# One grid operation ahead of the context's division on VectorE, and x's evictions swapped between VectorE and ScalarE

## The chip, the cores and the metric

The kernel runs on one core of a Trainium2 chip. The metric is the device time of one execution in microseconds, the median over the runs. Engines: TensorE (PE; PEld is its weight load), VectorE (DVE), ScalarE (ACT), GpSimd (POOL), and SyncE (SP), which here issues most DMAs.

## The reference

Four layers follow each other on x, 8 batches of 512 x 512 in float32. The change lies in the second, and moves operations of the first that run inside it:

```python
# L0: a finite-difference step on the 512 x 512 grid of each batch
df = -gradv_Af + gradvv_Bf * 0.5
f_new = jnp.maximum(f + df * dt[:, None, None], 0.0)
# L1: a transformer block, 16 heads of 32
x = _ln(src) * (1.0 + scale) + shift
scores = einsum(q / sqrt(32), k) + attention_bias, masked with -inf
ctx = einsum(softmax(scores), v)
x = x + (ctx @ Wo + bo);  h = _ln(x) * g2 + beta2
x = x + _gelu2(h @ W1 + b1) @ W2 + b2
# L2: an expert's MLP per batch with layer norm;  L3: a low-rank response, gated
```

## The kernel before

The program has three stages: the grid step of batch 0 (up to about 65 us), the attention of all batches (up to about 1165 us), and the MLPs with the low-rank layer. The change lies in the attention stage (`attention_stage`, lines 522 to 1097).

The attention works in 128 units (b, c, r): batch b, a group c of four heads, and a quarter r of the query rows (row index modulo 4). A batch has 16 units; the texts count them from 0 to 15 in their batch (t = 4c + r). The loop of line 1060 runs over units and overlaps three of them: `now` is in its softmax, `old` (the unit before) has its probabilities transposed, and `two` (the one before that) has its context summed. Every instruction of the compute engines is pinned to the order of the program, so that the order on an engine is that of the code; the bias loads on SyncE are not pinned and a scheduler places them.

What one turn of the loop issues, in order:

- on GpSimd a gate (L713), a tiny addition that reads the last grid operation's output and so holds GpSimd back until VectorE is through with the grid operations of the turn before; then two additions of the mask to the next unit's bias (L945);
- `turned` (L979) and `softmax` (L961), twice: transposes of the probabilities into a PSUM tile tr, copied to pt by VectorE (L993) for the first head and by ScalarE (L995) for the second; then on VectorE scores plus bias with the row minimum (bt, mn, L968), on ScalarE the exponential (L973). Between them lie pieces of the job that `fill` (L879) gives to this unit: a block of q, k, v or of the output projection, four matmuls at a time;
- the rest of the job. In unit 9 of a batch this holds `x1_in` (L578) four times, for the next batch: TensorE transposes a 128-column block c of the normalised x into a PSUM tile xtr, and it is evicted to SBUF as x1 with scale and shift, on ScalarE (L587) for even c and on VectorE (L589) for odd c;
- every fourth turn (units 1, 5, 9 and 13, for the head group that ended two units ago) `divide` (L1019): TensorE transposes the reciprocals of the sums (rb), ScalarE copies them out (rbs, L1024), VectorE multiplies the context with them (ct, L1027). Each turn then has `inverse` (L1012), the reciprocals of the unit `old` (rs on VectorE, rw on ScalarE);
- the bias loads three units ahead (L934), then the grid operations of this turn (`grid_sums`, L803), then the coefficient loads of the grid (`grid_loads`, L696) on SyncE;
- the score matmuls of the next unit (L950).

The tiles tr, xtr, rb and xb (the transposes back) share two PSUM banks (tag "tr"), so a transpose waits until an earlier tile of its bank has been evicted.

The grid step of batch n runs during batch n-1's attention, from its unit 8 on. Its place is a table by hand, `GRID` (L797): for each step j the names of the operations. A letter is a coefficient or an action and a digit the half (two of each partition's four rows): e0 multiplies the coefficient tile e of half 0 with f on VectorE, C0 adds c0 to the sum, and so on; each is a tensor_tensor of 128x1024 in SBUF (L664). Only n0 and n1 (the layer norm) put passes on ScalarE, two each (L791). Step j of batch n falls in turn i = 16(n-1) - 8 + j, so the turns with a division are the steps 1, 5, 9 and 13. The coefficients are loaded two to four units ahead: e0 at step -1, g0 at step 1, e1 at step 6, a1 at step 9.

Of the kernel before, what the change touches and what calls it, by code (L numbers as in the profile page):

```python
# [24 lines left out]
R = 4  # L25
# [496 lines left out]
def attention_stage(  # L522
# [13 lines left out]
    with ExitStack() as ctx:  # L536
# [9 lines left out]
        def tp(out, src):  # L546
            pin(nc.tensor.transpose(out, src, ident))  # L547
# [30 lines left out]
        def x1_in(b, c):  # L578
            tag, bufs = ("tr", 2) if b or c < 2 else (f"s{c}", 1)
            tr = ps.tile([P, R, P], F32, name=f"xtr_{b}_{c}", tag=tag, bufs=bufs)  # L580
            for r in range(R):
                tp(tr[:, r, :], xt[b][:, r, c * P : (c + 1) * P])
            t = io.tile([P, S], F32, name=f"x1_{b}_{c}", tag="x1", bufs=4)
            tv, trv = t.rearrange("f (p r) -> f p r", r=R), tr.rearrange("f r p -> f p r")
            g, h = sc1[:, c, b : b + 1], shift[:, c, b : b + 1]
            if c % 2 == 0:
                pin(nc.scalar.activation(tv, trv, AF.Identity, bias=h, scale=g))  # L587
            else:
                pin(nc.vector.tensor_scalar(tv, trv, g, h, ALU.mult, ALU.add))  # L589
            x1s[b, c] = t  # L590
# [117 lines left out]
        def grid_gate(i):  # L708

            t = gs.pop("last", None)  # L710
            if t is not None:
                g = small.tile([P, 1], F32, name=f"gate_{i}", tag="gate", bufs=2)
                pin(nc.gpsimd.tensor_tensor(g, t, t, ALU.add))  # L713

        def grid_ghosts(n):
            f = gs[n, "f"]
            m1 = small.tile([P, R, 2, 4], F32, name=f"m1_{n}", tag="gm1", bufs=1)
            m2 = small.tile([P, R + 2, 2, 3], F32, name=f"m2_{n}", tag="gm2", bufs=1)

            def times(out, x, y):  # L720
                pin(nc.vector.tensor_tensor(out, x, y, ALU.mult))

            for i in range(2):
                o = 508 * i
                times(m1[:, :, i, :], grid["gab"][:, :, i, :], f[:, 1 : R + 1, o : o + 4])
                o = 509 * i
                times(m2[:, :, i, :], grid["gte"][:, :, i, :], f[:, :, o : o + 3])
            e1 = small.tile([P, R, 2], F32, name=f"e1_{n}", tag="ge1", bufs=2)
            e2 = small.tile([P, R + 2, 2], F32, name=f"e2_{n}", tag="ge2", bufs=1)
            pin(nc.vector.tensor_reduce(e1, m1, AX.X, ALU.add))  # L730
            pin(nc.vector.tensor_reduce(e2, m2, AX.X, ALU.add))
            gv(e1, e1, e2[:, 2 : R + 2, :], ALU.add)
            gv(e1, e1, e2[:, 0:R, :], ALU.subtract)
            gs[n, "ghost"] = e1

        def grid_op(n, op):
# [46 lines left out]
            elif key == "n":  # L783
# [5 lines left out]
                for r in range(2):  # L789
# [4 lines left out]
                        )  # L794
                    )

        GRID = {  # L797
            0: "q0 q1", 1: "e0", 2: "w0 c0 hh", 3: "C0", 4: "+0 -0", 5: "g0", 6: "G0 a0",
            7: "A0 b0 B0", 8: "x0 q2", 9: "e1 w1 c1", 10: "C1 +1", 11: "-1 g1", 12: "G1 s0",
            13: "n0 a1 A1 b1", 14: "B1 x1", 15: "s1", 16: "n1",  # L800
        }

        def grid_sums(n, j):  # L803
            for op in GRID.get(j, "").split():
                if op == "hh":
                    grid_ghosts(n)
                else:
                    grid_op(n, op)
# [6 lines left out]
        def grid_step(i, f):  # L815
            for n in range(1, NB):
                j = i - (16 * (n - 1) - 8)
                if -2 <= j <= 16:
                    f(n, j)
# [55 lines left out]
        def grid_early(j):  # L875
            grid_sums(1, j)
            grid_loads(1, j)
# [63 lines left out]
        def add_mask(b, c, r):  # L941
            for u in range(2):
                bt = bias[b, c, r, u]
                pin(
                    nc.gpsimd.tensor_tensor(  # L945
                        bt, bt, mask[b, r][:, None, :].to_broadcast([P, 2, S]), ALU.add
                    )
                )
# [12 lines left out]
        def softmax(b, c, r, u):  # L961

            bt = bias[b, c, r, u]
            for i in range(2):
                h = 2 * u + i
                mn = small.tile([P, 1], F32, name=f"mn_{b}_{c}_{r}_{h}", tag=f"mn{h}")
                pin(
                    nc.vector.tensor_tensor_reduce(  # L968
                        bt[:, i, :], ss[h], bt[:, i, :], -1.0, 3.0e38, ALU.add, ALU.min, mn
                    )  # L970
                )
                pin(
                    nc.scalar.activation(  # L973
                        bt[:, i, :], bt[:, i, :], AF.Exp, bias=mn, scale=-1.0,
                        accum_out=sums[b, c, r][:, h : h + 1],
                    )
                )

        def turned(b, c, r, u):  # L979

            bt = bias.pop((b, c, r, u))
            for i in range(2):
                h = 2 * u + i
                if r % 2 == 0:
                    pts[b, c, r // 2, h] = pp.tile(
                        [P, KC, 2, P], F32, name=f"pt_{b}_{c}_{r}_{h}", tag=f"pt{h}", bufs=1
                    )
                pt = pts[b, c, r // 2, h]
                tr = ps.tile([P, KC, P], F32, name=f"tr_{b}_{c}_{r}_{h}", tag="tr", bufs=2)
                for k in range(KC):  # L990
                    tp(tr[:, k, :], bt[:, i, k * P : (k + 1) * P])
                if i == 0:
                    pin(nc.vector.tensor_copy(pt[:, :, r % 2, :], tr))  # L993
                else:
                    pin(nc.scalar.copy(pt[:, :, r % 2, :], tr))  # L995

        def values(b, c, g):

            if g == 0:
                ctxs[b, c] = ps.tile([P, R, P], F32, name=f"ctx_{b}_{c}", tag="ctx")  # L1000
            cx = ctxs[b, c]
            p4 = [pts.pop((b, c, g, i)) for i in range(4)]
            for k in range(KC):
                for i in range(4):
                    h = 4 * c + i
                    mm(
                        cx[i * HD : (i + 1) * HD, 2 * g : 2 * g + 2, :],
                        vs[b, k][:, h * HD : (h + 1) * HD], p4[i][:, k, :, :],
                        k == 0, k == KC - 1,
                    )  # L1010

        def inverse(b, c, r):  # L1012
            rs = small.tile([P, 4], F32, name=f"rs_{b}_{c}_{r}", tag="rs")
            pin(nc.vector.reciprocal(rs, sums.pop((b, c, r))))
            rw = pp.tile([P, 4, HD], F32, name=f"rw_{b}_{c}_{r}", tag="rw", bufs=4)
            pin(nc.scalar.copy(rw, rs[:, :, None].to_broadcast([P, 4, HD])))
            sums["w", b, c, r] = rw
# [15 lines left out]
        def drain(jobs):  # L1033
            for _ in jobs:
                pass
# [3 lines left out]
        n = len(units)  # L1039
# [6 lines left out]
        for c in range(KC):  # L1046
            x1_in(0, c)
# [12 lines left out]
        for i in range(n + 2):  # L1060
            now = units[i] if i < n else None
            old = units[i - 1] if 1 <= i <= n else None
            two = units[i - 2] if i >= 2 else None
            jobs = fill(now[0], 4 * now[1] + now[2]) if now else iter(())
            grid_gate(i)
            if i + 1 < n:
                add_mask(*units[i + 1])
            grid_step(i - 1, grid_pow)
            pair = two and two[2] % 2 == 1
            if pair:  # L1070
                values(two[0], two[1], two[2] // 2)
            for u in range(2):
                if old:
                    turned(*old, u)
                if now:
                    softmax(*now, u)
                next(jobs, None)
            drain(jobs)
            if pair and two[2] == R - 1:
                divide(two[0], two[1])  # L1080
            if old:
                inverse(*old)
            if i + 3 < n:
                load_bias(*units[i + 3])
            if now and now[0] == NB - 1:
                head_load(4 * now[1] + now[2])
            if now and now[0] and now[1:] == (2, 1):
                nc.sync.dma_start(x1d[now[0] - 1], xt[now[0] - 1])
            grid_step(i, grid_sums)
            grid_step(i, grid_loads)  # L1090
            if i + 1 < n:
                scores(*units[i + 1])
# [723 lines left out]
```

## Time and profile before

| | |
|---|---|
| median of 3 runs | 2859.53 us (2859.52 to 2860.22) |
| the profiled execution | 2864.53 us, span 2862.8 us, mean granted clock 0.986 |
| busy: PE, DVE, ACT, POOL | 96%, 68%, 35%, 52% of the span |
| in 300 to 400 us (attention): PE, DVE, ACT, POOL | 95.9, 84.3, 64.2, 54.3 us of 100 |
| in 1300 to 1400 us (MLP): PE, DVE, ACT, POOL | 100.0, 65.0, 20.2, 58.4 us of 100 |
| division ct (L1027) | x32, 692 ns each |
| x's evictions: ACT L587, DVE L589 | 777 ns and 810 ns each, x16 each |
| DVE copies pt (L993) | x256, 687 ns each |

The profile is one execution on the chip. A row of its list of groups has the line, the engine and operation, the tiles (out<-in), the shape and the count; then the busy time in us and the mean in ns; then the engine's idle time just before these instructions, and what ended it. In a timeline, the first two numbers are the start and the length in us, and the bracket at the end is the engine's idle time before the instruction and the releaser. Matmul ends are modelled, so a busy TensorE is not one at its peak. The granted clock is the share of TensorE's full clock.

### The profile page before, as it was taken

To read this page: it belongs to the slowest core of one execution; us is meant where nothing else is said; L and a number is where in the kernel's file an instruction comes from. 1 tells how busy PE (TensorE), PEld (TensorE's weight loads), DVE (VectorE), ACT (ScalarE), POOL (GpSimd) and SP (SyncE) were. 2 spreads that over 40 slices of the span, in tenths; PEclk is the share of its full clock that TensorE was granted. 3 is DMA by queue.
4 is the path that set the end of the run, shared out by engine and by line. 5 is a ranking of instruction groups with operands and counts; after the bars stand their busy time and mean duration, and the time that the engine had idled before them with its cause. 6 is when DMAs were issued, how large, how long until landed. Compare 5 with 4: busy or idle time off the path is not lost.

```text
span 2862.8 us, 39706 instructions
## 1 busy us (share of the span) xinstructions
PE 2738.6 (96%) x14606; PEld 2008.5 (70%) x14606; DVE 1945.2 (68%) x3606; ACT 1002.7 (35%) x2133; POOL 1495.7 (52%) x1062
## 2 busy tenths in 40 slices
PE   5889999999999999999999999999999999999997
PEld 2455545454545555688888888887888888888885
DVE  7788888888888766576566656664456555656554
ACT  1366666666666666212111211211121121121221
POOL 2345455555555655366465555654545545545632
PEclk9999999999999999999999999999999999999998
DMA  8655656565666555433532444253133133143120
GB/s 306 210 192 178 218 170 230 167 229 171 224 203 207 162 159 184 165 100 81 154 122 61 127 138 123 49 166 112 59 110 126 52 141 125 49 144 111 41 74 30
DMA packets 190352, 405.60 MB, mean 142 GB/s; under 512 B 24321, under 2 KB 28993, under 8 KB 183631
## 3 DMA queue, kind: packets, MB, share of 16 engines
q1 hardware_dynamic: 185170, 391.94, 41.0%
q0 software_dynamic: 3680, 11.07, 3.1%
q8 instruction: 116, 1.90, 0.3%
q14 instruction: 78, 0.63, 0.1%
q10 hardware_dynamic: 1308, 0.07, 0.0%
HBM read 367.32 MB, written 31.50 MB: 139 GB/s over the span
## 4 chain that ended last, share of the span: by engine, by line
PE 79%; DVE 14%; ACT 4%; DMA 2%; issue 1%; POOL 0%; SPq 0%; ACTq 0%; DVEq 0%; POOLq 0%
PE u L1129 27%; PE y L1129 24%; PE tr L547 6%; PE ctx L544 4%; PE s L544 4%; PE o L544 3%; PE pv L544 3%; PE pq L544 2%; DVE x L664 2%; DVE bt L968 2%; ACT bt L973 2%; DVE pt L993 2%; PE pk L544 2%; DVE tb L1135 1%; DVE act L1135 1%
## 5 line engine op out<-in xcount | busy, mean ns | idle before, releaser
L1129 PE MATMUL y<-wo,act 128*128 128x256 f32 x2560 | 578.9, 381 | 0.0
L945 POOL TENSOR_TENSOR bt<-bt,mk 128x1024 f32<-128x1024 f32 x256 | 541.8, 2138 | 58.8 <-DMA bt<-in_bias 42.6
L1129 PEld LDWEIGHTS y<-wo,act 128*128 128x128 f32 x2560 | 479.4, 190 | 82.2 <-issue 20.5
L973 ACT ACTIVATE bt<-bt,mn 128x512 f32<-128x512 f32 x512 | 365.5, 715 | 137.0 <-DVE mn L968 136.7
L547 PEld LDWEIGHTS tr<-ident,bt 128*128 128x128 f32 x2048 | 229.1, 142 | 189.7 <-issue 118.6
L1129 PE MATMUL u<-bt,wi 128*128 128x256 f32 x1440 | 332.4, 381 | 0.0
L968 DVE CUSTOM_DVE_ANT_0 bt<-s,bt 128x512 f32<-128x512 f32 x512 | 330.5, 683 | 0.0
L547 PE MATMUL tr<-ident,bt 128*128 128x128 f32 x2048 | 282.7, 280 | 38.8 <-DVE pt L993 27.7
L1135 DVE TENSOR_TENSOR act<-u,u 128x512 f32<-128x512 f32 x256 | 173.4, 687 | 212.8 <-PE u L1129 138.0
L1129 PEld LDWEIGHTS u<-bt,wi 128*128 128x128 f32 x1440 | 274.6, 191 | 37.6
L993 DVE COPY pt<-tr 128x512 f32<-128x512 f32 x256 | 175.9, 687 | 100.4 <-PE tr L547 99.7
L1129 PE MATMUL u<-tb,ws 128*128 128x256 f32 x1024 | 242.4, 380 | 0.0
L1129 PE MATMUL y<-t,s 128*128 128x256 f32 x1024 | 234.1, 380 | 0.0
L1129 PEld LDWEIGHTS u<-tb,ws 128*128 128x128 f32 x1024 | 195.1, 191 | 26.7
L995 ACT COPY pt<-tr 128x512 f32<-128x512 f32 x256 | 148.2, 579 | 183.9 <-PE tr L547 181.5
L1138 POOL TENSOR_TENSOR t<-wo,t 128x512 f32<-128x512 f32 x64 | 104.5, 1648 | 198.2 <-PE y L1129 198.2
L1129 PEld LDWEIGHTS y<-t,s 128*128 128x128 f32 x1024 | 190.6, 190 | 23.8
L1135 DVE TENSOR_TENSOR x<-y,x 128x512 f32<-128x512 f32 x96 | 64.5, 686 | 183.2 <-PE y L1129 129.2
L1441 ACT ACTIVATE act<-act,bi 128x512 f32<-128x512 f32 x128 | 83.9, 712 | 292.3 <-DVE act L1135 292.2
L1441 ACT ACTIVATE act<-act,b 128x512 f32<-128x512 f32 x128 | 82.9, 712 | 292.4 <-DVE act L1135 292.4
L1135 DVE TENSOR_TENSOR u<-u,u 128x512 f32<-128x512 f32 x192 | 131.3, 684 | 59.5 <-PE u L1129 59.5
L544 PE MATMUL s<-kt,qt 32*128 32x512 f32 x1024 | 166.9, 644 | 2.1 <-DVE mn L968 1.1
(315 smaller groups left out, 4283.2 us busy)
## 6 DMA issues: line engine op xcount, KB each, us to landing
bt<-in_bias SPq DMA_DIRECT2D x256, 512.0 KB
wo<-in_W SPq DMA_DIRECT2D x32, 1024.0 KB
wi<-in_Wi SPq DMA_DIRECT2D x32, 1024.0 KB
wo<-in_Wo_e SPq DMA_DIRECT2D x32, 1024.0 KB
wi<-in_W SPq DMA_DIRECT2D x28, 1024.0 KB
gq<-coef_q SPq DMA_DIRECT2D x21, 512.0 KB
x1d<-x SPq DMA_DIRECT2D x8, 1024.0 KB
x<-x1d SPq DMA_DIRECT2D x8, 1024.0 KB
```

The costliest lines, as they stand in the source:

```text
L544: pin(nc.tensor.matmul(out, lhsT=lhsT, rhs=rhs, start=start, stop=stop))
L547: pin(nc.tensor.transpose(out, src, ident))
L664: pin(nc.vector.tensor_tensor(out, x, y, op))
L945: nc.gpsimd.tensor_tensor(bt, bt, mask[b, r][:, None, :].to_broadcast([P, 2, S]), ALU.add)
L968: nc.vector.tensor_tensor_reduce(bt[:, i, :], ss[h], bt[:, i, :], -1.0, 3.0e38, ALU.add, ALU.min, mn)
L973: nc.scalar.activation(bt[:, i, :], bt[:, i, :], AF.Exp, bias=mn, scale=-1.0, accum_out=sums[b, c, r][:, h : h + 1],)
L993: pin(nc.vector.tensor_copy(pt[:, :, r % 2, :], tr))
L995: pin(nc.scalar.copy(pt[:, :, r % 2, :], tr))
L1129: pin(nc.tensor.matmul(out, lhsT=lhsT, rhs=rhs, start=start, stop=stop))
L1135: pin(nc.vector.tensor_tensor(out, x, y, op))
L1138: pin(nc.gpsimd.tensor_tensor(out, x, y, op))
L1441: nc.scalar.activation(acts[g][:, k, :], acts[g][:, k, :], func, bias=bi[:, j : j + 1])
```

## The change

Two edits in the attention stage. First, x's evictions: odd c now goes to ScalarE and even c to VectorE, in all 8 batches. Second, a bar in the `GRID` table divides the steps 1, 5, 9 and 13. In a turn with a division, what is left of the bar (e0, g0, e1 or a1) is issued ahead of `divide`, the rest at the old place. In step 13 n0 stood first and now stands behind the bar, after a1. Where a step with a bar meets no division (the first batch's steps) the whole step is issued at the old place.

```diff
-            if c % 2 == 0:
+            if c % 2:
                 pin(nc.scalar.activation(tv, trv, AF.Identity, bias=h, scale=g))
             else:
                 pin(nc.vector.tensor_scalar(tv, trv, g, h, ALU.mult, ALU.add))
...
-            0: "q0 q1", 1: "e0", 2: "w0 c0 hh", 3: "C0", 4: "+0 -0", 5: "g0", 6: "G0 a0",
-            7: "A0 b0 B0", 8: "x0 q2", 9: "e1 w1 c1", 10: "C1 +1", 11: "-1 g1", 12: "G1 s0",
-            13: "n0 a1 A1 b1", 14: "B1 x1", 15: "s1", 16: "n1",
+            0: "q0 q1", 1: "e0 |", 2: "w0 c0 hh", 3: "C0", 4: "+0 -0", 5: "g0 |", 6: "G0 a0",
+            7: "A0 b0 B0", 8: "x0 q2", 9: "e1 | w1 c1", 10: "C1 +1", 11: "-1 g1", 12: "G1 s0",
+            13: "a1 | n0 A1 b1", 14: "B1 x1", 15: "s1", 16: "n1",
...
-        def grid_sums(n, j):
-            for op in GRID.get(j, "").split():
+        def grid_sums(n, j, late=True, early=True):
+            ops = GRID.get(j, "")
+            if "|" in ops and not (late and early):
+                ops = ops.split("|")[late]
+            elif not late:
+                ops = ""
+            for op in ops.replace("|", "").split():
...
-            if pair and two[2] == R - 1:
+            split = pair and two[2] == R - 1
+            if split:
+                grid_step(i, lambda n, j: grid_sums(n, j, late=False))
                 divide(two[0], two[1])
...
-            grid_step(i, grid_sums)
+            grid_step(i, lambda n, j: grid_sums(n, j, early=not split))
```

In the built program 25 of the 32 divisions have a grid operation moved ahead of them: a1 in 7, e0, g0 and e1 in 6 each. On VectorE that operation stands just before ct, where it stood two to three instructions behind it. On ScalarE only the evictions change places; TensorE's and GpSimd's orders stay as they were. On SyncE one pair changes places in five batches: the load of the coefficient g of half 0 stands ahead of the second bias load of unit 12, where it stood behind it.

## The prediction

> **What bounds the kernel now.** I read the page first: TensorE is busy 96% of the 2862.8 us, VectorE 68%. The change touches only the attention stage (about 120 to 1165 us), so the page's averages say little, and I went to the list of TensorE's idle times there, then to the chain of waits and the timeline around one division, and last to the granted clock. In one batch (16 units; 286 to 422 us) TensorE has seven idle stretches over 0.1 us, 6.02 us in all, in every batch the same: 0.70 and 1.24 after the division of unit 5 (counted in its batch from 0), 1.15 and 0.43 at x's transposes in unit 9, 0.24 after the division of unit 13, 0.32 two units later, 1.94 after the division of unit 1. First the groups: the division's multiply, its count, its mean, and VectorE's idle time before it.
>
> ```profile
> L1027 DVE TENSOR_TENSOR ct<-ctx,rbs 128x512 f32<-128x512 f32 x32 | 22.1, 692 | 52.0 <-ACT rbs L1024 52.0
> ```
>
> VectorE stands idle 1.6 us on average ahead of each division, until ScalarE's copy of the reciprocals arrives. Then the chain of waits at the division of unit 1 (start us, length us, what), and TensorE's timeline there:
>
> ```profile
> 387.57 0.69 DVE ct L1027
> 388.26 0.08 DVE rs L1014
> 388.34 1.11 DVE x L664
> 389.46 1.13 DVE gq L664
> 390.59 1.14 DVE gc L664
> 391.73 0.61 DVE pt L993
> 392.34 0.04 issue
> 392.38 0.66 PE tr L547 x4
> ```
>
> ```profile
> 389.85 0.60 PE L547 MATMUL tr<-ident,bt 128*128 128x128 f32 x4
> 392.38 0.66 PE L547 MATMUL tr<-ident,bt 128*128 128x128 f32 x4 [1.94 <-DVE pt L993]
> ```
>
> The wait that ends last is VectorE's list: division, reciprocal, three grid operations, and only then pt, which frees the PSUM bank that TensorE's fourth transpose needs. VectorE had been idle 2.02 us just before. Last, TensorE's work and clock in stretches of 3.41 us (length; PE, PEld, DVE, ACT, POOL busy; granted clock; DMA):
>
> ```profile
> 254.74:258.15 3.41, 1.47 (x8) 0.74 (x7) 3.41 (x5) 0.00 (x0) 0.74 (x2) 1.00 0.47 154
> 258.15:261.57 3.42, 3.42 (x8) 1.50 (x6) 2.75 (x9) 3.07 (x8) 3.42 (x2) 0.50 0.39 99
> 422.01:425.42 3.41, 1.68 (x7) 0.61 (x5) 3.38 (x4) 1.60 (x3) 0.31 (x2) 1.00 0.53 156
> 425.42:428.84 3.42, 3.21 (x15) 1.66 (x16) 3.42 (x11) 2.63 (x8) 3.42 (x2) 1.00 0.36 82
> ```
>
> A stretch with 1.94 us idle is followed by one at half clock; one with about 1.7 is not.
>
> **Moving the grid operation.** It happens at 25 of the 32 divisions; nothing is added, no DMA moves with it. One operation costs 1.11 to 1.14 us of VectorE in the chain (start to start).
> Unit 1 (6 times, e1). VectorE is free from 385.55, ct starts at 387.57: the operation fits in the 2.02 us with 0.8 to spare, ct starts as before, and pt 1.13 us earlier. TensorE's 1.94 falls to about 0.8. 6 x 1.13 = 6.8 us. The cover is the wait for ScalarE; were it gone, the move would be worth nothing.
> Unit 5 (7 times, a1). Same idle time, 2.02. The 1.24 falls to about 0.1; the 0.70 before it stays, since ScalarE runs n0's two passes (1.51 us, L791) ahead of its own pt, and n0 keeps its place behind ct. 7 x 1.13 = 7.9 us. What is late next here is ScalarE.
> Unit 13 (6 times, g0). Idle 1.13, about the length of the operation: ct up to 0.1 later, pt a microsecond earlier, but TensorE waits only 0.24. 6 x 0.24 = 1.4 us.
> Unit 9 (6 times, e0). TensorE doesn't wait for VectorE behind this division: nothing by itself.
> In units 9 and 13 it is also the unit's last grid operation, for which GpSimd's gate waits, so the mask additions begin 2 to 3 us earlier. That keeps them off unit 10's w0, which took 1.95 us against 1.21 elsewhere; VectorE has slack there, so I count nothing.
>
> **Swapping the evictions** (unit 9, 7 times). The timeline now:
>
> ```profile
> 320.30 0.81 DVE L589 TENSOR_SCALAR x<-xtr,sc,shift 128x512 f32<-128x512 f32 x1 [1.12 <-PE xtr L547]
> 320.59 0.76 ACT L587 ACTIVATE x<-xtr,shift,sc 128x512 f32<-128x512 f32 x1
> 321.41 1.09 PE L547 MATMUL xtr<-ident,x 128*128 128x128 f32 x8 [1.15 <-ACT x L587]
> ```
>
> ScalarE is held by exponentials and kt until 320.59, VectorE is free from 319.17. With the first block on VectorE its eviction runs from 319.78 (the first four of eight transposes that start at 319.22 and take 1.04) to 320.59, and TensorE goes on at 320.65 instead of 321.41. The second block's eviction by ScalarE still ends at 321.35, so the fourth block's transposes start at 321.41 and end near 322.0. The third goes to VectorE from 321.3 to 322.1, and rb, which needs its bank, starts at 322.16 instead of 322.94: 0.78 us. The fourth ends on ScalarE at 322.8, in time for rbs. The tail has no other TensorE wait until unit 13. 7 x 0.78 = 5.5 us. Bounds: 0 if ScalarE's second eviction comes so late that it sets rb, 1.58 if both waits vanish; I take the worked value. In the prologue the same swap delays a mask conversion by 1 us, under GpSimd's wait for loads: nothing.
>
> **The clock.** The batch from the division at 324.25 to that at 456.68 has no half-clock stretch and takes 132.43 us; 726.75 to 860.23 has one, 133.48; 189.78 to 324.25 has two, 134.47. So one costs 1.03 us. Six (at 258, 292, 559, 661, 695, 828 us) follow a stretch with 1.94 idle, made by units 1 and 5; these stretches keep 0.8 us idle. The Trainium skill (TensorE: Matmul & The Clock Gate, Why this matters for your kernels) asks only that idle gaps stay under about 3 us; by it no gap here can cost clock and nothing is to be had. The rows above show 1.94 us in one stretch to be enough. By the rule 0, by the row 6 x 1.03 = 6.2; I take the row.
>
> **Against the change.** The Trainium skill (SBUF — State Buffer, SBUF: two separate sides) says that GpSimd and a VectorE operation with two SBUF inputs exclude each other for whole instructions. The moved operations have two. In unit 1 GpSimd's additions end at 385.27, VectorE starts at 385.55: 0.28 us apart. By the rule an overlap holds the operation up for the rest of a 2.13 us addition; up to 0.8 us of that still lies in the idle time. The row decides: apart; counted 0, at most 1 us x 6.
> SyncE's order puts the load of g's first half one place ahead of a bias load in five batches. That bias load waited for its buffer (issued 317.81, the one ahead at 315.22), so I count 0; were it held up, GpSimd's longest wait for a bias load, 4.7 us, is the price each time.
>
> **Sum.** 6.8 + 7.9 + 1.4 + 5.5 + 6.2 = 27.8 us. The profiled execution took 2864.5 (span 2862.8), so it would take 2836.7; the runs' median is 5.0 lower: 2859.5 - 27.8 = 2831.7.
>
> **Rivals.**
> A: the clock still drops as often (the windows only shift): 27.8 - 6.2, so 2837.9. For it: a drop near 1121 follows little idle. Against: all six follow the same 1.94.
> B: another wait takes the place of pt. The score matmuls wait for VectorE too (41.2 us at their weight loads). If half of the gain is lost there: about 2846. Against: these waits come later on the same VectorE list, which moves whole.
> C: slower. A coefficient lands later than the operation's new place, about 2.7 us earlier, and the division stands queued behind it, with pt and everything on VectorE. Nothing shows when they land, only that no grid operation in this stage waited for one past start-up. If they land just before their present use, the idle time comes back and pt starts about 0.7 us later than now (unit 1: 388.26 + 1.20 for the operation + 0.61 + 0.08 for ct and rs + 1.13 + 1.14 for the other two = 392.4, against 391.73): 19 x 0.7 = 13, and the other seven of thirteen long stalls drop the clock (7.2), less 5.5 of the swap: +15, 2874. It decides once a load lands within 2 us of its present use. Against: e1 is issued at 360.49, used at 388.26.
> D: none of it reaches TensorE: 2859.
>
> **Chances.** Forecast 0.62, A 0.15, B 0.14, D 0.04, C 0.05. Within 0.2% (5.7 us, about what a measurement of this kernel tells from no change): 0.04; faster 0.91; slower 0.05. The range takes in A and B with two microseconds beyond, and below it the swap at its bound of 1.58 (7 x 0.8 = 5.6 more, 2826) with four for waits that I counted at nothing: 2822 to 2848. The forecast's own is 2826 to 2837.
>
> **What would show it.** VectorE's idle before ct near 0.8 in units 1 and 5 and near 0 in 13; TensorE's 1.94 down to 0.8, 1.24 to 0.1, 0.24 gone, 1.15 to 0.4; a batch of about 129.2 us; no half clock between 180 and 1000 us. Grid operations ahead of ct that wait for a DMA, or last over 1.3 us, would prove me wrong.

## The result and the profile after

The changed kernel takes 2832.99 us (median of 4 runs, 2832.02 to 2835.08); the kernel before 2859.88 (4 runs, 2859.52 to 2865.43). The ratio is 0.9902, 95% interval 0.9885 to 0.9920: 26.9 us or 0.98% faster. The profiled execution has a span of 2830.3 us against 2862.8, and the whole difference of 32.5 us arises in the attention stage: the last division starts at 1131.55 us instead of 1164.03.

The same views as before, of the kernel after. The division in the list of groups:

```profile
L1033 DVE TENSOR_TENSOR ct<-ctx,rbs 128x512 f32<-128x512 f32 x32 | 22.1, 692 | 27.0 <-ACT rbs L1030 27.0
```

VectorE's idle time ahead of it fell from 52.0 to 27.0 us. VectorE's timeline around the division of unit 1 (start, length; in brackets the idle time before and its releaser), and TensorE's behind it:

```profile
376.08 1.22 DVE L664 TENSOR_TENSOR x<-x,gf 128x1024 f32<-128x1024 f32 x1
378.18 0.69 DVE L1033 TENSOR_TENSOR ct<-ctx,rbs 128x512 f32<-128x512 f32 x1 [0.88 <-ACT rbs L1030]
378.79 0.17 DVE L1020 RECIPROCAL rs<-sums 128x4 f32<-128x4 f32 x1
378.87 1.20 DVE L664 TENSOR_TENSOR gq<-gq,gq 128x1024 f32<-128x1024 f32 x1
379.98 1.22 DVE L664 TENSOR_TENSOR gc<-gc,gf 128x1024 f32<-128x1024 f32 x1
381.12 0.69 DVE L999 COPY pt<-tr 128x512 f32<-128x512 f32 x1
```

```profile
380.46 0.60 PE L547 MATMUL tr<-ident,bt 128*128 128x128 f32 x4
381.86 0.65 PE L547 MATMUL tr<-ident,bt 128*128 128x128 f32 x4 [0.80 <-DVE pt L999]
```

e1 now runs in what was idle time, 0.88 us of it are left, and ct still starts as soon as rbs is there. pt comes one operation sooner behind ct, and TensorE's wait is 0.80 instead of 1.94. TensorE's waits behind the division of unit 5, first in the kernel before (division at 420.62), then after (at 410.10):

```profile
423.76 0.63 PE L547 MATMUL tr<-ident,bt 128*128 128x128 f32 x4 [0.70 <-ACT pt L995]
425.63 0.66 PE L547 MATMUL tr<-ident,bt 128*128 128x128 f32 x4 [1.24 <-DVE pt L993]
```

```profile
413.24 1.26 PE L547 MATMUL tr<-ident,bt 128*128 128x128 f32 x8 [0.71 <-ACT pt L1001]
```

The wait for VectorE's pt is gone and the one for ScalarE's stays; all eight transposes now follow each other. The evictions of unit 9:

```profile
310.91 1.04 PE L547 MATMUL xtr<-ident,x 128*128 128x128 f32 x8
311.55 0.81 DVE L589 TENSOR_SCALAR x<-xtr,sc,shift 128x512 f32<-128x512 f32 x1 [0.69 <-PE xtr L547]
312.28 0.76 ACT L587 ACTIVATE x<-xtr,shift,sc 128x512 f32<-128x512 f32 x1
312.41 1.34 PE L547 MATMUL xtr<-ident,x 128*128 128x128 f32 x8 [0.47 <-DVE x L589]
...
313.97 0.66 PE L547 MATMUL rb<-ident,rw 128*128 128x128 f32 x4 [0.22 <-DVE x L589]
```

TensorE waits 0.47 and 0.22 us there instead of 1.15 and 0.43. The batch that follows, from division to division (length; PE, PEld, DVE, ACT, POOL busy; granted clock):

```profile
315.29:444.26 128.97, 126.43 (x820) 69.16 (x816) 112.94 (x245) 83.86 (x200) 71.17 (x50) 1.00 0.63 204
```

All six batches between 186 and 960 us take 128.97 to 128.99 us and have the full clock; before they took 132.4 to 135.6. There is no half-clock stretch left between 161 and 1089 us.

### The profile page after: what moved, and what is told of

Its sections match the earlier page's. It is cut to its first block, busy times and chain, and to the rows that moved or that the text cites. A ratio compares the mean times of both kernels' runs of the same rounds, so it can differ in the third digit from the quotient of the medians.

```text
span 2830.3 us, 39706 instructions
## 1 busy us (share of the span) xinstructions
PE 2730.7 (96%) x14606; PEld 2005.4 (71%) x14606; DVE 1940.9 (69%) x3606; ACT 1003.7 (35%) x2133; POOL 1495.7 (53%) x1062
## 4 chain that ended last, share of the span: by engine, by line
PE 82%; DVE 13%; ACT 2%; issue 1%; DMA 1%; POOL 0%; ACTq 0%; SPq 0%; DVEq 0%; POOLq 0%
PE u L1137 27%; PE y L1137 24%; PE tr L547 6%; PE s L544 4%; PE ctx L544 4%; PE o L544 3%; PE pv L544 3%; PE pq L544 3%; PE pk L544 2%; DVE bt L974 2%; DVE x L664 2%; DVE pt L999 1%; DVE tb L1143 1%; ACT bt L979 1%; DVE act L1143 1%
```

## The experiments

Runs of one group shared a chip and the runs of the kernel before on it; the median of the kernel before was 2861.3 us in the first group, 2860.3 in the second and in the third. Ratios are to the kernel before. "Batch" is the time from the division of unit 9 to that of the next batch, in the profiled execution; batches with a half-clock stretch or another disturbance are named apart.

**The edits one by one.** First x's evictions alone:

```diff
-            if c % 2 == 0:
+            if c % 2:
                 pin(nc.scalar.activation(tv, trv, AF.Identity, bias=h, scale=g))
```

> Only x's evictions are swapped. My theory (each edit removes its own TensorE waits, and they add up): 7 times (1.15 + 0.43 - 0.47 - 0.22) = 6.2 us less than before, about 2853.7; TensorE's waits at x's transposes 0.47 and 0.22; 1.94 and 1.24 behind the divisions of units 1 and 5 stay, and with them half-clock stretches. Rival (the swap pays only together with the moved operation, because the division still comes late): about 2860, no difference.

Measured: 2858.69 us, ratio 0.9988 (0.9981 to 0.9994): 2.6 us less by the medians, 1.7 to 5.4 by the interval. The waits are 0.47 and 0.22 as expected, but the batch without disturbance shrinks only from 132.44 to 131.79, by 0.65 where the waits shrink by 0.89. So the swap pays by itself, and less than both I and the expectation gave it: 7 x 0.65 = 4.6 us. Half-clock stretches remain (290, 389, 423, 556, 659, 956 us).

Then the grid operations alone (the `GRID` table and the split, evictions as before):

> Only the grid operations are moved. My theory: the whole gain of 26.9 less the swap's 6.2, so about 2839; 1.94 falls to 0.8, 1.24 and 0.24 to nothing, no half-clock stretch between 180 and 1000 us, the waits at x's transposes stay at 1.15 and 0.43. In unit 9 e0 makes ct 0.3 us late, with no TensorE wait from it. Rival (the swap carries most of it, the moved operation only shifts VectorE's idle time): above 2850.

Measured: 2839.95 us, ratio 0.9917 (0.9904 to 0.9930), 21.3 us less. Undisturbed batch 129.61, 2.83 less than before; TensorE's waits 0.80 behind unit 1, none but ScalarE's 0.70 behind unit 5, 1.15 and 0.43 at x's transposes; no half-clock stretch between 162 and 1097 us. In unit 9 e0 makes ct 0.16 us late, and no TensorE wait comes of it. 0.65 + 2.83 = 3.48, and the two together measured 132.44 - 128.98 = 3.46: the edits add up, and the rival, which left most to the swap, falls.

The moved operations by pairs: with the bar in front (`"| e0"`, `"| g0"`) only e1 and a1 move, with `"| e1 w1 c1"` and `"| n0 a1 A1 b1"` only e0 and g0; evictions as before.

> Only e1 and a1 are moved (units 1 and 5), evictions as before. My theory: all of the moved operations' gain but the 1.4 us of unit 13, so about 2840.5, and no half-clock stretch. Rival (all four kinds give alike, 25 operations of 1.1 us each shared out evenly): 13 of 25 of the gain, about 2849.

> Only e0 and g0 are moved (units 9 and 13), evictions as before. My theory: 6 x 0.24 = 1.4 us, about 2858.4, the long waits behind units 1 and 5 and the half-clock stretches as before, although as many VectorE microseconds move into idle time as in the run with e1 and a1. Rival (even shares): 12 of 25, about 2850.

Measured: e1 and a1 alone 2842.23 us, ratio 0.9927 (0.9915 to 0.9939), batch 130.04, no half-clock stretch between 163 and 1098 us. e0 and g0 alone 2861.47 us, ratio 0.9995 (0.9987 to 1.0004), not to be told from no change; the only undisturbed batch is 131.84, and half-clock stretches stand at 290, 423, 556, 689 and 822 us. Both pairs put about as many VectorE microseconds into idle time; only where pt held TensorE did that pay. Even shares are out. That batch starts at a division that e0 makes 0.16 us late and ends at one without e0, the last batch having no grid step to run; set against the kernel before by TensorE's transposes it is 0.44 us shorter, so 132.00 and not 131.84. Of the 0.44, 0.40 arise where TensorE waited 0.24 behind unit 13: with the wait gone, the first transpose also starts 0.16 before the modelled end of the matmul ahead of it. And 2.40 + 0.44 = 2.84 is the 2.83 of the four together.

**The clock by itself.** The kernel before, with more TensorE work inside the long waits and nothing else:

```diff
-                for k in range(KC):
+                again = 3 if u == 1 and i == 0 and r == 1 and c < 2 and b < NB - 1 else 1
+                for k in list(range(KC)) * again:
                     tp(tr[:, k, :], bt[:, i, k * P : (k + 1) * P])
```

> The kernel before, with four transposes of the third head issued three times instead of once in units 2 and 6 (behind the divisions of units 1 and 5), into the same PSUM tile with the same values: about 1.04 us more of TensorE work inside waits of 1.94 us (all but the last batch). Nothing moves on VectorE. My theory (the half-clock stretches come from the idle time in a stretch of 3.41 us): no half-clock stretch between 180 and 1000 us any more, every batch near 132.4 us, and some 3 to 6 us less than before. Rival (transposes do not count as work for the clock gate, or the idle time is not the cause): half-clock stretches as before, the time as before.

Measured: 2855.77 us, ratio 0.9982 (0.9974 to 0.9989): 4.5 us less by the medians, 3.1 to 7.4 by the interval, for doing more. TensorE behind the division of unit 1, and three batches:

```profile
385.06 1.47 PE L547 MATMUL tr<-ident,bt 128*128 128x128 f32 x12
387.60 0.66 PE L547 MATMUL tr<-ident,bt 128*128 128x128 f32 x4 [1.06 <-DVE pt L994]
```

```profile
319.46:451.89 132.43, 128.17 (x836) 70.85 (x832) 113.38 (x245) 83.52 (x200) 71.12 (x49) 1.00 0.62 202
451.89:584.32 132.43, 128.18 (x836) 70.85 (x832) 113.37 (x246) 83.52 (x200) 71.13 (x49) 1.00 0.62 205
584.32:716.74 132.42, 128.16 (x836) 70.83 (x832) 113.37 (x246) 83.51 (x200) 71.19 (x49) 1.00 0.62 201
```

Twelve transposes stand where there were four, the idle time is 1.06, and the next transposes start when VectorE lets them, as before. No batch loses clock: all six take 132.42 or 132.43, to be set against 132.44 for an undisturbed batch before. In all 16 timed runs the mean granted clock is 0.99 or more, in the 20 of the kernel before beside them at most 0.989. So the half clock came from TensorE's idle time. With it gone, the moved operations and the swap are left with the rest, 2855.8 to 2833.0.

**What is late next.** Two variants of the changed kernel and both together:

```diff
-            7: "A0 b0 B0", 8: "x0 q2", 9: "e1 | w1 c1", 10: "C1 +1", 11: "-1 g1", 12: "G1 s0",
+            7: "A0 b0 B0", 8: "x0 q2", 9: "e1 w1 | c1", 10: "C1 +1", 11: "-1 g1", 12: "G1 s0",
...
-            13: "a1 | n0 A1 b1", 14: "B1 x1", 15: "s1", 16: "n1",
+            13: "a1 | A1 b1", 14: "n0 B1 x1", 15: "s1", 16: "n1",
```

> The changed kernel, with w1 moved ahead of the division of unit 1 as well. My theory (VectorE's list behind ct still sets the 0.80 wait there): two operations, 2.25 us, overrun the 2.02 us by about 0.25, pt comes 0.85 earlier, the 0.80 goes: 6 x 0.8 = 4.8 us less than the changed kernel, a batch of about 128.2. Rival (the second operation only makes ct late): no gain.

> The changed kernel, with n0 (two passes on ScalarE) moved from step 13 to the start of step 14. My theory (the 0.70 left behind the division of unit 5 is ScalarE's pt behind n0's passes): the 0.70 goes, 7 x 0.7 = 4.9 us less than the changed kernel, a batch of about 128.3. Rival (the passes cost the same in the next unit, ahead of its pt and of x1's rectifier): no gain.

> The changed kernel with both: w1 ahead of the division of unit 1, n0 in step 14. My theory: the two add up, 9.7 us less than the changed kernel, a batch of about 127.5, about 2823. Rival (one of them exposes the next wait): as the better of the two single runs.

Measured: w1 ahead too, 2827.66 us (ratio to the kernel before 0.9879, 0.9864 to 0.9894), 5.3 less than the changed kernel by the medians; the two intervals still touch, but the undisturbed batch went from 128.98 to 128.0 (128.2 was expected). The 0.80 behind unit 1 is gone and a wait of 0.35 stands four transposes earlier; another half microsecond came from the unit's score matmuls, which start sooner. n0 in step 14, 2836.17 us (0.9907, 0.9891 to 0.9922): no gain, undisturbed batch 128.97; and not for the rival's reason. TensorE behind unit 5 there:

```profile
417.57 0.66 PE L547 MATMUL tr<-ident,bt 128*128 128x128 f32 x4 [0.80 <-DVE pt L999]
```

ScalarE's 0.70 is gone, and VectorE's pt, which had been late by as much but hidden under it, is now what TensorE waits for. The profile before had a sign of it: the two waits behind unit 5, 0.70 + 1.24, make the 1.94 of unit 1, so 1.13 less on VectorE's list leaves 0.8 in both places. w1 ahead and n0 later together, 2826.16 us (0.9882, 0.9867 to 0.9897), batch 128.0: as w1 alone. So my theory of unit 5 was half right, and the next run takes VectorE's side with it:

```diff
-            13: "a1 | n0 A1 b1", 14: "B1 x1", 15: "s1", 16: "n1",
+            13: "a1 A1 | b1", 14: "n0 B1 x1", 15: "s1", 16: "n1",
```

> w1 ahead of the division of unit 1, n0 in step 14, and A1 ahead of the division of unit 5 too. My theory (with n0 out of the way it is VectorE's pt at 0.80 that TensorE waits for behind unit 5, hidden until now under the 0.70 of ScalarE): A1 overruns the 2.02 us by about 0.4 and pt comes 0.7 to 0.8 earlier; 7 x 0.7 = 5 us less than with w1 alone (2827.7), about 2822.5, a batch near 127.3. Rival (ct's delay is what counts there): as with w1 alone.

Measured: 2819.99 us (0.9853, 0.9830 to 0.9875), batch 127.15, TensorE's wait behind unit 5 0.48. This beats both kernels: 13 us below the changed one by the medians, and the intervals lie apart.

**Batches that lose 2 us.** In some executions single batches take about 2.05 us longer than the half clock accounts for: 131.69 and 131.70 in the run with the grid operations alone, 132.13 in that with e1 and a1, 130.06 in that with w1, 131.02 and 131.04 in that with n0 later, one each in the swap alone and in e0 and g0 alone, and one of the kernel before (135.58, which is 132.44, a half-clock stretch and 2.1). VectorE's timeline in that batch of the kernel before:

```profile
572.39 0.69 DVE L779 BATCH_NORM_STATS2 gst<-x 128x6 f32<-128x512 f32 x1 [0.37 <-DMA x<-xed]
573.12 0.18 DVE L780 BATCH_NORM_AGGREGATE gmv<-gst 128x2 f32<-128x6 f32 x1
573.34 2.06 DVE L781 TENSOR_SCALAR grs<-gmv 128x2 f32<-128x2 f32 x1
575.31 0.68 DVE L993 COPY pt<-tr 128x512 f32<-128x512 f32 x1
```

The DMA of the grid's edge row (operation x1) lands 0.37 us late, and the layer norm's addition of epsilon (L781), to two numbers per partition, then takes 2.06 us: it ends at 575.40, when a run of GpSimd's mask additions (2.1 us each) ends at 575.38. In all nine batches this addition took 2.06 to 2.16 us, in the other batches between 180 and 1000 us 0.17 to 0.48. The row was 0.19 to 0.37 us late in eight of the nine; in the ninth VectorE waited less than 0.1. The test puts that addition on GpSimd:

```diff
-                pin(nc.vector.tensor_scalar(rs, mv[:, :, 1], LN_EPS, None, ALU.add))
+                pin(nc.gpsimd.tensor_scalar(rs, mv[:, :, 1], LN_EPS, None, ALU.add))
```

> The changed kernel, with the tiny addition of the layer norm's epsilon (128x2, L781) on GpSimd instead of VectorE. My theory (some batches lose 2.05 us because this addition on VectorE comes a little late, behind x1's edge row, and then waits for a whole 2.1 us mask addition of GpSimd): no batch is 2 us longer than the others any more, the timed runs lie closer together, the fastest as before: about 2832. Rival (the delay is the edge row's DMA itself): batches of 131 us still occur.

> Both of these together. My theory: about 2822, every batch alike near 127.3, timed runs within some 2 us. Rival: batches 2 us longer still occur in some runs.

Measured: on the changed kernel 2832.30 us (0.9895, 0.9871 to 0.9919), batches 128.80 to 128.82; with all the rest 2819.09 us (0.9851, 0.9827 to 0.9874), batches 126.92 to 126.93 but for one of 127.05. In that one the row was late again:

```profile
674.73 0.69 DVE L779 BATCH_NORM_STATS2 gst<-x 128x6 f32<-128x512 f32 x1 [0.31 <-DMA x<-xed]
675.45 0.18 DVE L780 BATCH_NORM_AGGREGATE gmv<-gst 128x2 f32<-128x6 f32 x1
675.55 0.66 DVE L999 COPY pt<-tr 128x512 f32<-128x512 f32 x1
675.72 0.22 POOL L781 TENSOR_SCALAR grs<-gmv 128x2 f32<-128x2 f32 x1 [2.20 <-DVE gmv L780]
```

A lateness of 0.31 us now costs the batch 0.12, not 2.05: the loss was the wait for GpSimd, not the DMA. This one batch is what tells: four profiles without the edit have no long batch either. The timed runs did not come closer together (2829.4 to 2835.2, and 2817.7 to 2822.9), so their spread has another source as well, which stays open, and the medians don't differ from those without this edit. That source need not be the clock: with more transposes, the times spread from 2851.4 to 2858.9 at a mean clock of 0.99.

## Why the prediction was right

It said 2831.7 and the time is 2833.0; the gain was 27.8 us by the sum and 26.9 by the medians. The mechanism was right; that the sum came within 1 us is in part luck, since a batch gained more than worked out and the clock less, and the interval of the gain reaches from 22.9 to 32.9. Its steps:

- **Unit 1**: ct at its old place, 0.8 us spare, pt 1.13 earlier, the 1.94 down to 0.8. Measured: 0.88 spare, 0.80.
- **Unit 5**: 1.24 down to 0.1, ScalarE's 0.70 stays. Measured so. But ScalarE was not alone: with its passes gone VectorE's pt gives 0.80. Units 1 and 5 together measured 132.44 - 130.04 = 2.40 a batch, where the sum had 2.26.
- **Unit 13**: the 0.24 went, and e0 was to bring nothing. The pair measured 0.44 a batch; this term was too small, by 6 x 0.2 = 1.2 us, since the wait that went gave back 0.40 where its idle time was 0.24.
- **The swap**: 0.78 a batch was worked out, 0.65 measured alone (and 129.61 - 128.98 = 0.63 on top of the grid operations). Too large by about 1 us in all: four transposes were counted as half of eight, 0.52 us, but four alone take 0.60 (the row at 380.46), and VectorE's eviction waits for four of them twice.
- **The clock**: counted by the rows of the profile, not by the rule of the Trainium skill (TensorE: Matmul & The Clock Gate, Why this matters for your kernels) that idle gaps only have to stay under about 3 us: here 1.94 us in one stretch were enough. The run with more transposes measured it at 4.5 us by the medians, against 6.2; the interval holds both. 6.2 was read off one execution with six such stretches, and their number changes from run to run: the swap alone met six, e0 and g0 alone five.
- **GpSimd's exclusion**: the moved operations stayed clear of it (e1 1.22 us, and ct never late but for what the forecast said). What it did not foresee is that a wait for GpSimd costs 2.05 us elsewhere, in some batches, and for an operation with one SBUF input (L781), where it had looked at those with two. The earlier gate did what was said: w0 took 1.95 us at most before and 1.20 after, without a gain of its own that shows.
- **SyncE's swapped loads** and **rival C**: no moved operation waited for a DMA between 180 and 1000 us.
- **From profile to median**: the sum was made against a profiled execution of 2864.5, and from profile to profile the kernel gained 32.5, not 27.8. The difference: 0.18 a batch more than worked out (6 x 0.18 = 1.1), the one batch with the late edge row (2.1), and the first 186 us, which gained 3.47 where 1.13 + 0.78 stood in the sum (a seventh half-clock stretch, at 169 us, went too). The kernel before ran from 2858.5 to 2867.4 us on the first group's chip; its profiled execution was one of the longer ones. The medians agree with the sum better than the profiles do.

Rival A (the clock drops as often) falls with the trace after and the run with more transposes; B (another wait takes pt's place) with 3.46 a batch; D with the result. That another engine hides behind the one that a wait names was true in unit 5, where it cost the follow-up its first try.

## What to carry to other kernels

Idle time of an engine ahead of an instruction that waits for another engine is a free slot, but filling it pays only where what stands behind that instruction holds up the bound engine: about the same number of moved microseconds gave 2.40 us a batch in two places and 0.44 in two others. When two engines hand back the buffers of a pair in turn, the wait that the profile names can cover a second one of the same length, so take both away before judging either. And where the profile shows half-clock stretches, count the engine's idle time in the stretch before each: here a wait of 1.94 us that fell into one stretch cost 1 us more than its length six times, and shortening it to 0.8 brought back both.

## What the runs showed of the hardware

- Between 180 and 1000 us, TensorE's clock fell to half for 3.41 us when the stretch of 3.41 us before had about 1.93 us of idle time or more. Added up over stretches aligned with the drops, in the kernel before, in the swap alone and in e0 and g0 alone, all 17 drops follow 1.93 to 1.95 us, the largest without one are 1.90, 1.76 and 1.75 us, and a single stretch of 1.94 has none. Repeated transposes were enough to prevent it.
- Idle time is not all of it. Outside that range the kernel before has drops at 132 and 169 us behind 0.64 us of idle time and at 1122 us behind 1.00, and the swap alone one at 1123 us behind 0.09. What sets these off stays open.
- One such stretch costs about 1.0 us of the batch (133.48 against 132.44; 132.72 to 132.86 against 131.79 in the swap alone; 133.06 against 132.00 in the run with e0 and g0), less than the 1.7 us that half a stretch would be.
- A VectorE operation on two numbers per partition (L781) took 0.17 to 2.16 us beside GpSimd's additions, 0.22 on GpSimd itself: it ends with the addition in progress, and being 0.2 to 0.4 us late can cost a whole one.
